# Sums of a graph layer's messages at every second step alone, two rounds in one burst, ahead of the second layer

## The chip, the core and the metric

The kernel runs on one core of a Trainium2 chip. Its five engines matter here: TensorE (PE; its weight loads are shown apart as PEld), VectorE (DVE), ScalarE (ACT), GpSimd (POOL) and SyncE (SP, which issues DMAs). The metric is the time of one execution on the device, in microseconds (us).

## The reference

One message-passing layer of a graph network over 6,250 nodes of 128 features and 100,000 edges, then a layer norm of x plus its result. All numbers are float32.

```python
row, col = (edge_index[0], edge_index[1])            # edges sorted by col
msg_in = jnp.concatenate([node_features[row], node_features[col]], axis=-1)
h = jax.nn.relu(msg_in @ Wm1 + bm1)                  # 256 -> 256
h = jax.nn.relu(h @ Wm2 + bm2)                       # 256 -> 256
messages = h @ Wm3 + bm3                             # 256 -> 128
agg = segment_sum(messages, col); count = segment_sum(1, col)
agg = agg / jnp.clip(count, 1.0)[:, None]
node_in = jnp.concatenate([node_features, agg], axis=-1)
upd = jax.nn.relu(node_in @ Wn1 + bn1) @ Wn2 + bn2
x = _layernorm(x + node_features + upd)
```

## The kernel before

Before the loop, x is multiplied by the upper half of Wm1 into a table in memory (`atab`, a row per node), and its lower half's product becomes another one (`btab`). The 100,000 edges are cut into 196 groups of 512, four tiles of 128 edges each. A loop goes over steps k, one group a step, with these parts:

- `gather` (L533): POOL fetches the rows of `atab` for group k+2 with four indirect DMAs, indices in `srcT`, for odd groups in `srcP`. The `rows` tile has four buffers, so the gather of group g follows the transposes of group g-4. The index copy `pace(k+5)` at the end of an even step (L893, DVE) fills `srcP`, and the odd gather waits for it.
- `first_layer` (L569, L582): PE transposes the gathered rows into two PSUM banks (16 instructions, 64 rows each) and adds the destination's terms by one-hot matmuls. ACT applies bias and relu (L588, four instructions) into `h1`.
- `make_hot` (L547, L552; DVE, even steps): one-hot tables for the next two groups; `oh` places an edge in a window of 32 nodes.
- `second_layer` of group k-1 (L596): 16 PE instructions into two banks, and behind each a DVE instruction (L598) that writes h2. There are six h2 buffers (`x_sb`, `h_more` in the profile).
- `node_step` (L694 to L745): from step 94 on, finished nodes go through the update and the layer norm in pieces, a piece in five stages, one stage a step: PE L700, L715, L719, L727; DVE L694 and L695 (a reciprocal), L702, L704, L706, L730, L734, L735, L741, L743; ACT L722, L737, L745.
- `some_sums` (L604): a one-hot times h2, 32 rows a window, four windows in four column groups of PE at once: one round is eight PE instructions. The last round of a bank is followed by a copy to SBUF on ACT (`part`, L609).
- `turn_sums`: PE turns such a part (L617, three instructions into a bank), DVE loads the windows' first nodes (L627) and adds the windows to the accumulator `acc` in SBUF (L624).

How many tiles share a window differs by region: four tiles in groups 0 to 71 ("quads": four groups to a bank, four rounds), two in groups 72 to 147 ("pairs": two groups, two rounds), one in 148 to 183 ("singles": a group, one round), four again in 184 to 191, two in the last four. `deal` writes down at which step a round is due, the turn one step after the last round.

PSUM has eight banks: seven go round as `bank`, one (`p3`, named `sum_bank`) holds the sums. The order on PE, ACT and DVE is that in which the code is written (a schedule by hand); a wait at the head of an engine's queue holds up all behind it. The loop's body has the parts in this order: first layer, gather, one-hots, second layer of the group before, node stage, turns and adds, sums, and at even steps the index copy.

Of the kernel before, what the change touches and what calls it, by code (L numbers as in the profile page):

```python
# [10 lines left out]
F32 = mybir.dt.float32  # L11
# [9 lines left out]
P = 128  # L21
# [15 lines left out]
def kernel(  # L37
# [39 lines left out]
    H = wm1.shape[1]  # L77
# [4 lines left out]
    NG = -(-E // GE)  # L82
# [16 lines left out]
    GL = NG - 2 * LATE  # L99
# [199 lines left out]
    with tc.tile_pool(name="prep", bufs=1) as prep, tc.tile_pool(name="pp", bufs=3, space=PSUM) as pp, tc.tile_pool(  # L299
        name="pb", bufs=5, space=PSUM  # L300
# [10 lines left out]
        with tc.high_priority():  # L311
# [7 lines left out]
            t = 4  # L319
            for n in (4, 8, 8, 8, 8, 8):  # L320
                n = min(n, NTF - t)
# [193 lines left out]
    with edge, tc.tile_pool(name="wk", bufs=2) as wk, tc.tile_pool(  # L515
        name="banks", bufs=7, space=PSUM
# [7 lines left out]
        def bank():  # L524
            return banks.tile([P, 2, H], F32, name="bank")

        def flat_bank():
            return bank().rearrange("p t h -> p (t h)")
# [16 lines left out]
        def hot_rows(rb):  # L545
            oht = wk.tile([P, 2, HE], BF16, name="oht")
            nc.vector.tensor_scalar(oht, rb, iota_p, None, op0=ALU.is_equal)  # L547
            return oht
# [58 lines left out]
        def part_of(pg, nw):  # L607
            part = wk.tile([P, H + 1], F32, name="part")
            nc.scalar.copy(part[:nw * WN], pg[:nw * WN, :H + 1])  # L609
            return part  # L610
# [26 lines left out]
        def nk_of(g):  # L637
            return 1 if g < 2 * HALVES or g >= GL else 2

        def make_hot(p):  # L640
            ohts[p] = hot_rows(rels[p // 2][:, 2 * (p % 2):2 * (p % 2) + 2])
            make_nodes(p)

        def make_nodes(p):
            ohs[p] = hot_nodes(dloc[:, 2 * p:2 * p + 2, :].rearrange("p g j -> p (g j)"), 2, iota_n)

        def units_of(g):
            q, n = g // 2, wide_of[g]
            tiles = [(ohs[q][:, g % 2, j, :], h2s[g % len(h2s)][:, j, :]) for j in range(NTS[g])]
            return [tiles[j:j + n] for j in range(0, NTS[g], n)]  # L650
# [104 lines left out]
        ohs, ohts, rels = {}, {}, {}  # L755
        rounds, turns_at, added = {}, {}, {}

        def deal(gs, n, steps):

            steps = list(steps)  # L760
            for t, k in enumerate(steps):
                rounds.setdefault(k, []).append((gs, t, n))
            at = steps[-1] + 1
            turns_at.setdefault(at, []).append(gs[0])
            added.update({g: at + 1 for g in gs})

        for r0, r1, n in REGIONS:
            m = min(n, GT)
            for g in range(2 * r0, 2 * r1, m):
                if n == GT:  # L770
                    deal(range(g, g + n), n, (g + 4, g + 5, g + 6, g + 6))
                elif n == 1:
                    deal([g], n, (g + 3,))
                elif r1 == PAIRS:
                    deal(range(g, g + n), n, (g + 3, g + 4))
                elif g + n < NG:
                    deal(range(g, g + n), n, (NG - 1, NG - 1))
        deal([NG - 2], 2, (NG, NG))
        deal([NG - 1], 2, (NG + 1, NG + 1))

        B_STEPS = B_FROM + 2 * (NT - B_EARLY) + 2
        begins, step = {}, B_STEPS
# [7 lines left out]
        sum_banks, parts = {}, {}  # L790

        def some_sums(k):

            for gs, t, n in rounds.pop(k, ()):
                windows = [w for g in gs for w in units_of(g)]
                if t == 0:
                    sum_banks[gs[0]] = flat_bank() if k > NG else p3.tile([P, 2 * H], F32, name="sum_bank")
                sum_tile(sum_banks[gs[0]], windows, t, n)
                if t == n - 1:
                    parts[gs[0]] = part_of(sum_banks.pop(gs[0]), len(windows)), len(windows)  # L800

        def turn_sums(k):
            for g in turns_at.pop(k, ()):
                part, nw = parts.pop(g)
                pt = turned(part, nw)
                add_up(pt, load_bases(uniti[0:1, unit_at[g]:unit_at[g] + nw], nw, ENG.DVE))
# [50 lines left out]
        for g in range(-4, NG + 14, 2):  # L857
            for i in range(g + 4, min(g + 6, NG)):
                terms[i] = fetch(load_bases(tilei[0:1, i * GT:(i + 1) * GT], NTS[i], ENG.SP), nk_of(i))
            if g < -2:  # L860
                continue
            if (g + 2) % 4 == 0 and g + 6 < NG:
                rels[(g + 6) // 4] = places((g + 6) // 4)
            if g < 0:
                continue
            if g == 0:
                first_step()
            for k in (g, g + 1):
                if k < NG:
                    s = st[k] = {}  # L870
                    if k == 1:
                        xts[1] = open_layer(None, NTS[1], xts[1])
                    s["h1"] = first_layer(rows.pop(k, None), terms.pop(k), ohts[k // 2][:, k % 2], NTS[k], nk_of(k),
                                          xts.pop(k, None))
                    if k == 0:
                        next_rows()
                    if k == 2:
                        nc.scalar.copy(*pace(5))
                if 2 * XS <= k + 2 < NG:
                    rows[k + 2] = gather(sources(k + 2))  # L880
                if k % 2 == 0 and k + 2 < NG:
                    make_hot(k // 2 + 1)
                if 0 <= k - 1 < NG:
                    second_layer(st.pop(k - 1)["h1"], h2s[(k - 1) % len(h2s)], NTS[k - 1])
                if k < NG:
                    node_step(k)
                if k <= NG:
                    turn_sums(k)
                some_sums(k)
                if k > NG:  # L890
                    turn_sums(k)
                if k % 2 == 0 and 2 <= k and k + 5 < NG:
                    nc.vector.tensor_copy(*pace(k + 5))  # L893
                if k >= NG:
                    node_step(k)
            if g < 6:
                clear(8)
            if g == 0:
                more_rows()
            t0 = B_EARLY + (g - B_FROM) // 2  # L900
            if g >= B_FROM and (g - B_FROM) % 4 == 0 and t0 < NT:
                pbt = bank()
                for a in range(min(2, NT - t0)):
                    nc.tensor.matmul(pbt[:, a, :], xT[:, (t0 + a) * P:(t0 + a + 1) * P], w1[:, 1, :],  # L904
                                     start=True, stop=True)
                b_terms(t0, pbt, b_rows, b_rest)
            if g == 18:
                late_weights()
            if g == 60:
                made_weights()  # L910
            if g == NG + 2:
                with tc.high_priority():
                    again = nc.values_load(
                        again_i[0:1, 0:1], min_val=0, max_val=1,
                        skip_runtime_bounds_check_because="0 or 1, by its computation")
# [77 lines left out]
```

## Time and profile before

| | |
|---|---|
| runs of the kernel before | 1333.75, 1343.81, 1348.66 us; median 1343.81 |
| the profiled execution | 1338.36 us, span 1336.6 us, TensorE clock 0.981 |
| PE busy | 1236.1 us, 92% of the span |
| DVE, ACT, POOL busy | 618.2 (46%), 441.9 (33%), 748.7 us (56%) |
| L596 on PE | 768.7 us in 3128 instructions |
| L604 on PE | 104.1 + 59.1 us in 1044 + 512 instructions |
| L617 on PE, L624 on DVE | 47.3 us in 291, 96.7 us in 382 |

In the profile a group's row has: line, engine, operation, output<-inputs, count | busy time, mean ns of one | idle time of the engine just before them and what ended it ("issue": nothing that the trace shows). A timeline's row has: start, length (of so many instructions one after the other), engine, line, operation, and in brackets the idle time before it. Starts of one engine's successive rows, taken from each other, give a price that holds the overlap between instructions.

### The profile page before, as it was taken

How to read it: one execution, taken by the hardware profiler on the slowest of the kernel's cores; microseconds unless marked ns; L12 is line 12 of the kernel's file. 1: busy time of each engine (PE TensorE's matmuls, PEld its weight loads, DVE VectorE, ACT ScalarE, POOL GpSimd, SP SyncE). 2: the span in 40 equal slices, each digit the busy share in tenths (PEclk: the TensorE clock that was granted, in tenths of full speed). 3: DMA queues.
4: the chain of work that ended last, by engine and by line, in shares of the span. 5: the costliest groups of instructions: out<-in, count | busy, mean ns of one | idle time of the engine just before them, and what ended most of it. 6: DMA issues, size and time to landing. Idle time of an engine off the chain costs nothing.

```text
span 1336.6 us, 27771 instructions
## 1 busy us (share of the span) xinstructions
PE 1236.1 (92%) x10031; PEld 925.5 (69%) x10032; DVE 618.2 (46%) x1551; ACT 441.9 (33%) x1102; POOL 748.7 (56%) x795
## 2 busy tenths in 40 slices
PE   9779998998999999999899999999999999999997
PEld 7556666666666666676677777777777777777675
DVE  6443333433334333434466554444445556556553
ACT  4432323323323323333333423333233333333331
POOL 2366665665665666656555465565655555555550
PEclk9879999999999999999999999999999999999998
DMA  8544434444434434434444344444444434443330
GB/s 287 177 125 134 132 108 127 130 115 129 133 106 128 135 107 125 134 106 131 126 118 119 114 125 128 118 120 129 118 118 118 115 109 118 109 123 110 106 91 4
DMA packets 107617, 163.90 MB, mean 123 GB/s; under 512 B 26367, under 2 KB 71549, under 8 KB 107457
## 3 DMA queue, kind: packets, MB, share of 16 engines
q0 software_dynamic: 37504, 102.29, 27.7%
q1 hardware_dynamic: 69425, 59.50, 14.0%
q8 instruction: 82, 1.34, 0.4%
q14 instruction: 62, 0.51, 0.1%
q10 hardware_dynamic: 544, 0.26, 0.1%
HBM read 142.48 MB, written 19.86 MB: 121 GB/s over the span
## 4 chain that ended last, share of the span: by engine, by line
PE 89%; issue 7%; DVE 2%; another core or an unknown queue 1%; DMA 1%; ACT 0%; SPq 0%; DVEq 0%
PE bank L596 54%; PE bank L569 9%; PE sum_bank L604 9%; PE bank L582 4%; PE bank L617 2%; PE pbt L431 2%; PE bank L727 2%; PE bank L700 2%; PE bank L719 2%; PE bank L715 2%; PE bank L904 1%; PE pt L448 0%; DVE acc L660 0%; DVE x_sb L598 0%
## 5 line engine op out<-in xcount | busy, mean ns | idle before, releaser
L596 PE MATMUL bank<-w,h 128*128 128x256 f32 x3128 | 768.7, 392 | 67.2 <-issue 64.6
L596 PEld LDWEIGHTS bank<-w,h 128*128 128x128 f32 x3128 | 581.7, 192 | 212.3 <-issue 131.1
L533 POOL DMA_INDIRECT rows<-atab,srcT x392 | 374.9, 956 | 260.6 <-issue 90.4
L533 POOL DMA_INDIRECT rows<-atab,srcP x384 | 364.2, 949 | 277.9 <-issue 126.5
L588 ACT ACTIVATE h<-bank,b 128x256 f32<-128x256 f32 x782 | 306.5, 476 | 395.6 <-remote 189.3
L598 DVE TENSOR_TENSOR x_sb<-bank,nb 128x512 f32<-128x512 f32 x263 | 181.0, 691 | 401.7 <-PE bank L596 233.7
L598 DVE TENSOR_TENSOR h_more<-bank,nb 128x512 f32<-128x512 f32 x128 | 88.3, 692 | 177.5 <-PE bank L596 75.0
L569 PEld LDWEIGHTS bank<-ident,rows 64*128 64x128 f32 x3096 | 112.7, 140 | 77.7 <-issue 56.8
L569 PE MATMUL bank<-ident,rows 64*128 64x64 f32 x3096 | 139.3, 230 | 0.0
L624 DVE TENSOR_TENSOR acc<-acc,bank 128x96 f32 x382 | 96.7, 253 | 51.7 <-PE bank L569 16.5
L604 PE MATMUL sum_bank<-x_sb,oh 128*32 128x257 f32 x1044 | 104.1, 393 | 3.0 <-issue 1.6
L609 ACT COPY part<-sum_bank 128x257 f32<-128x257 f32 x96 | 35.8, 373 | 197.0 <-PE bank L582 75.4
L582 PE MATMUL bank<-oht,terms 64*128 64x128 bf16 (+1 forms) x1132 | 82.6, 237 | 14.5 <-issue 10.9
L604 PE MATMUL sum_bank<-h_more,oh 128*32 128x257 f32 x512 | 59.1, 391 | 1.2 <-DVE h_more L598 0.6
L604 PEld LDWEIGHTS sum_bank<-x_sb,oh 128*32 128x32 f32 x1044 | 28.1, 108 | 41.7 <-issue 34.1
L582 PEld LDWEIGHTS <-terms 64*128 64x128 bf16 x1132 | 44.1, 97 | 16.1 <-issue 13.8
L617 PE MATMUL bank<-ident,part 128*128 128x128 f32 (+1 forms) x291 | 47.3, 271 | 0.5 <-ACT part L609 0.5
L745 ACT ACTIVATE y<-y,sh,rs 128x128 f32<-128x128 f32 (+3 forms) x50 | 22.1, 487 | 67.0 <-DVE sh L743 26.6
L695 DVE RECIPROCAL x_sb<-x_sb 128x256 f32<-128x256 f32 (+3 forms) x26 | 43.0, 1655 | 0.9
L617 PEld LDWEIGHTS bank<-ident,part 128*128 128x128 f32 (+1 forms) x291 | 36.6, 139 | 9.3 <-ACT part L609 1.0
L552 DVE TENSOR_TENSOR oh<-iota_n,dloc 128x256 f32<-128x256 f32 x98 | 40.8, 417 | 3.6 <-ACT dloc L838 3.6
L737 ACT ACTIVATE sd<-mv,eps 128x2 f32<-128x2 f32 (+3 forms) x26 | 7.7, 295 | 97.6 <-DVE mv L735 49.5
(157 smaller groups left out, 625.0 us busy)
## 6 DMA issues: line engine op xcount, KB each, us to landing
terms<-btab SPq DMA_DIRECT2D x566, 32.0 KB
places<-reltab SPq DMA_DIRECT2D x98, 128.0 KB
btab<-x_sb SPq DMA_DIRECT2D x10, 768.0 KB
rows<-atab,srcT POOLq DMA_INDIRECT x392
atab<-acc SPq DMA_DIRECT2D x12, 512.0 KB
rows<-atab,srcP POOLq DMA_INDIRECT x384
xr<-in_x_dram SPq DMA_DIRECT2D x23, 128.0 KB
out_dram<-y SPq DMA_DIRECT2D x23, 128.0 KB
```

The costliest lines, as they stand in the source:

```text
L533: nc.gpsimd.indirect_dma_start(out=ag[:, j, :], out_offset=None, in_=atab[:, :], in_offset=bass.IndirectOffsetOnAxis(ap=idx[:, j:j + 1], a ...
L552: nc.vector.tensor_tensor(oh[:, :ng].rearrange("p g j n -> p (g j) n"), iota.to_broadcast([P, ng * GT, WN]), dl.rearrange("p (j o) -> p j ...
L569: nc.tensor.matmul(ph[h][:, c, u * NQ:(u + 1) * NQ], ag[halves[h], u, c * P:(c + 1) * P], ident[halves[h], halves[h]], is_transpose=True, ...
L582: nc.tensor.matmul(ph[h][:, c, k * n:(k + 1) * n], bw[halves[h], k, c * P:(c + 1) * P], oht[halves[h], k * n:(k + 1) * n], start=False, st ...
L588: nc.scalar.activation(h1[:, c, h * HE:(h + 1) * HE], ph[h][:, c, :], AF.Relu, bias=b1[:, c:c + 1])
L596: nc.tensor.matmul(ph2[:, j - j0, :], h1[:, c, j * P:(j + 1) * P], w2[:, c, :], start=(c == 0), stop=(c == HC - 1))
L598: nc.vector.tensor_tensor(h2[:, j0:j0 + 2, :H], ph2, nb2.to_broadcast([P, 2, H]), op=ALU.max)
L604: nc.tensor.matmul(pg[w * WN:(w + 1) * WN, :H + 1], oh, h2, start=(t == 0), stop=(t == total - 1), skip_group_check=True)
L609: nc.scalar.copy(part[:nw * WN], pg[:nw * WN, :H + 1])
L617: nc.tensor.matmul(pt[:, c, :q], rows, ident[:q, :q], is_transpose=True, start=True, stop=True, skip_group_check=True)
L624: nc.vector.tensor_add(window, window, pt[:, :, j * WN:(j + 1) * WN])
L695: nc.vector.reciprocal(rc, rc)
```

## The change

Three things change. The due steps of the rounds: in quads the four rounds move from steps g+4, g+5, g+6, g+6 to g+5, g+5, g+7, g+7 (in the late quads g+5, g+5, g+6, g+6); in pairs both are at g+3; in singles an even group's round stays at g+3, an odd group's comes a step earlier, so that two singles are summed at the same odd step. The second of these takes one of the seven `bank`s ("beside") where all singles had `sum_bank`, as does the last group of all. And turns with their adds, then sums, stand ahead of the second layer and the node stage of the step.

```diff
-        def deal(gs, n, steps):
+        def deal(gs, n, steps, beside=False):
...
-                rounds.setdefault(k, []).append((gs, t, n))
+                rounds.setdefault(k, []).append((gs, t, n, beside))
...
                 if n == GT:
-                    deal(range(g, g + n), n, (g + 4, g + 5, g + 6, g + 6))
+                    deal(range(g, g + n), n, (g + 5, g + 5, g + 7, g + 7) if g < GL else (g + 5, g + 5, g + 6, g + 6))
                 elif n == 1:
-                    deal([g], n, (g + 3,))
+                    deal([g], n, (g + 3 - g % 2,), g % 2 == 1)
                 elif r1 == PAIRS:
-                    deal(range(g, g + n), n, (g + 3, g + 4))
+                    deal(range(g, g + n), n, (g + 3, g + 3))
...
-        deal([NG - 1], 2, (NG + 1, NG + 1))
+        deal([NG - 1], 2, (NG + 1, NG + 1), True)
...
-                    sum_banks[gs[0]] = flat_bank() if k > NG else p3.tile([P, 2 * H], F32, name="sum_bank")
+                    sum_banks[gs[0]] = flat_bank() if beside else p3.tile([P, 2 * H], F32, name="sum_bank")
...
+                if k <= NG:
+                    turn_sums(k)
+                some_sums(k)
                 if 0 <= k - 1 < NG:
                     second_layer(st.pop(k - 1)["h1"], h2s[(k - 1) % len(h2s)], NTS[k - 1])
                 if k < NG:
                     node_step(k)
-                if k <= NG:
-                    turn_sums(k)
-                some_sums(k)
```

On PE, in the singles at steps 164 and 165, this stood in a row before (x8 behind L596 and x4 behind L604 count written matmuls, each two instructions in the profile; `sum_bank` and `bank` are PSUM banks, `h_more` and `x_sb` are h2):

```order
L596 MATMUL bank<-w_151,h_13544 128x256 x8
L715 MATMUL bank<-xT,wu_159 128x2x2x64 x2
L719 MATMUL bank<-x_sb,wu_159 128x256 x2
L617 MATMUL bank<-ident,part 128x128 x3
L604 MATMUL sum_bank<-h_more,oh 32x257 x4
L569 MATMUL bank<-ident,rows 128x64 x16
L582 LDWEIGHTS terms
L582 MATMUL bank<-oht,terms 128x128
...
L596 MATMUL bank<-w_151,h_13650 128x256 x8
L727 MATMUL bank<-wu_160,x_sb 128x128 x4
L617 MATMUL bank<-ident,part 128x128 x3
L604 MATMUL sum_bank<-x_sb,oh 32x257 x4
```

Now, at steps 163 and 164:

```order
L604 MATMUL sum_bank<-h_more,oh 32x257 x4
L604 MATMUL bank<-h_more,oh 32x257 x4
L596 MATMUL bank<-w_151,h_13474 128x256 x8
L715 MATMUL bank<-xT,wu_159 128x2x2x64 x2
L719 MATMUL bank<-x_sb,wu_159 128x256 x2
L569 MATMUL bank<-ident,rows 128x64 x16
L582 LDWEIGHTS terms
L582 MATMUL bank<-oht,terms 128x128
...
L617 MATMUL bank<-ident,part 128x128 x6
L596 MATMUL bank<-w_151,h_13567 128x256 x8
L727 MATMUL bank<-wu_160,x_sb 128x128 x4
```

Two bursts of one round have become one burst of two, ahead of L596 at the odd step; both turns stand ahead of L596 at the even step. The whole order has 175 bursts of L604 before and 99 now: 18 fewer in the first quads, 38 in the pairs, 18 in the singles, 2 in the late quads.

On DVE, in the singles, an even step before (step 164; the index copy L893 is its last instruction, the four pairs of an ISA register instruction and an addition are cut to one):

```order
L598 TENSOR_TENSOR x_sb<-bank,nb_155 128x2x256 x2
L706 SCALAR_TENSOR_TENSOR xr<-xr,bu_161 128x256
L627 TENSOR_LOAD starts_i
L624 ISA
L624 TENSOR_TENSOR acc<-acc,bank 128x3x32
...
L893 COPY srcP<-srcT 128x4
```

And now, where eight additions are cut to two:

```order
L547 TENSOR_SCALAR oht<-places,iota_p 128x512
L552 TENSOR_TENSOR oh<-iota_n,dloc 128x256
L627 TENSOR_LOAD starts_i
L624 ISA
L624 TENSOR_TENSOR acc<-acc,bank 128x3x32
...
L598 TENSOR_TENSOR x_sb<-bank,nb_155 128x2x256 x2
L730 TENSOR_TENSOR y<-xr,bank 128x256
L734 BN_STATS stats<-y 128x6
L735 BN_AGGR mv<-stats 128x2
...
L893 COPY srcP<-srcT 128x4
```

The additions have moved from behind the node stage, next to L893, to the front of the step, ahead of L598; L893 follows L598 and what the node stage of the step issues. The odd step's additions are gone.

More of the change, by code (lines that the diff above doesn't have):

```diff
@@ L792, in some_sums @@
         def some_sums(k):
-            for gs, t, n in rounds.pop(k, ()):
+            for gs, t, n, beside in rounds.pop(k, ()):
                 windows = [w for g in gs for w in units_of(g)]
                 if t == 0:
-                    sum_banks[gs[0]] = flat_bank() if k > NG else p3.tile([P, 2 * H], F32, name="sum_bank")
+                    sum_banks[gs[0]] = flat_bank() if beside else p3.tile([P, 2 * H], F32, name="sum_bank")
                 sum_tile(sum_banks[gs[0]], windows, t, n)
```

## The prediction

> **What bounds the kernel now.** I read the page first: busy shares, the chain that ended last, the costliest groups.
>
> ```profile
> PE 1236.1 (92%) x10031; PEld 925.5 (69%) x10032; DVE 618.2 (46%) x1551; ACT 441.9 (33%) x1102; POOL 748.7 (56%) x795
> ...
> PE 89%; issue 7%; DVE 2%; another core or an unknown queue 1%; DMA 1%; ACT 0%; SPq 0%; DVEq 0%
> ...
> L596 PE MATMUL bank<-w,h 128*128 128x256 f32 x3128 | 768.7, 392 | 67.2 <-issue 64.6
> ```
>
> TensorE works 1236.1 of 1336.6 us, and 67.2 us of its idle time lies in front of the second layer, L596. That looks like a kernel bound by PE alone. The windows by stage show that it is not so everywhere. The columns are span, PE, weight loads, DVE, ACT and POOL, each with its count.
>
> ```profile
> 300.00:500.00 200.00, 187.01 (x1477) 132.52 (x1476) 74.58 (x163) 62.81 (x153) 122.55 (x130) 0.99 0.42 123
> 712.00:768.00 56.00, 54.08 (x464) 43.01 (x463) 32.95 (x89) 20.80 (x56) 28.73 (x32) 1.00 0.41 118
> 768.00:985.00 217.00, 204.14 (x1802) 157.74 (x1802) 104.40 (x259) 69.40 (x182) 129.21 (x136) 1.00 0.44 122
> 1040.00:1290.00 250.00, 235.85 (x2017) 184.67 (x2015) 139.33 (x377) 85.07 (x225) 142.53 (x151) 1.00 0.40 112
> ```
>
> A gather is four DMA_INDIRECT on POOL, so 300 to 500 us holds 130/4 = 32.5 gathers, 6.15 us each; 712 to 768 us holds 8, 7.0 us each; 768 to 985 us holds 34, 6.38 us each; 1040 to 1290 us holds 37.75, 6.62 us each. The third view asks what POOL waited for, by stage: even groups gather with srcT, odd ones with srcP.
>
> ```profile
> L533 POOL DMA_INDIRECT rows<-atab,srcT x66 | 62.6, 949 | 38.7 <-issue 15.2 <-remote 11.7 <-PE bank L596 10.4
> L533 POOL DMA_INDIRECT rows<-atab,srcP x64 | 60.5, 946 | 39.0 <-issue 14.6 <-remote 12.8 <-PE bank L596 10.0
> ...
> L533 POOL DMA_INDIRECT rows<-atab,srcT x31 | 29.4, 947 | 18.8 <-issue 7.3 <-PE bank L582 4.8 <-DVE x_sb L702 3.4
> L533 POOL DMA_INDIRECT rows<-atab,srcP x30 | 28.4, 945 | 32.8 <-issue 21.4 <-PE bank L582 11.3
> ...
> L533 POOL DMA_INDIRECT rows<-atab,srcT x76 | 72.0, 948 | 45.5 <-issue 17.4 <-PE bank L596 9.7 <-PE bank L582 9.5
> L533 POOL DMA_INDIRECT rows<-atab,srcP x75 | 71.4, 952 | 62.2 <-issue 37.9 <-PE bank L596 15.9 <-PE bank L582 5.0
> ```
>
> The first pair is 300 to 500 us, the second 660 to 768, the third 1040 to 1290. Idle time per gather: 38.7/16.5 = 2.35 and 39.0/16 = 2.44 us in the first; 18.8/7.75 = 2.43 and 32.8/7.5 = 4.37 in the second; 45.5/19 = 2.39 and 62.2/18.75 = 3.32 in the third. About 2.4 us is there whatever the stage; with 3.8 us of work it gives a floor of some 6.15 us a group. So POOL sets the pace in the early stage (PE has 6% to spare), PE in 712 to 768 us (54.08/56 = 96.6% busy), and in the last one neither: PE is 94.3% busy, and the odd gathers come 0.9 us late. The timeline there says why.
>
> ```profile
> 1086.88 0.69 DVE L598 TENSOR_TENSOR x_sb<-bank,nb 128x512 f32<-128x512 f32 x1 [0.96 <-issue]
> 1087.49 0.42 DVE L706 SCALAR_TENSOR_TENSOR xr<-xr,bu 128x256 f32<-128x256 f32 x1
> ...
> 1088.41 0.49 PE L617 MATMUL bank<-ident,part 128*128 128x128 f32 x3
> ...
> 1089.03 0.95 POOL L533 DMA_INDIRECT rows<-atab,srcT  x1 [0.30 <-issue]
> ...
> 1091.29 0.25 PE L582 MATMUL bank<-oht,terms 64*128 64x128 bf16 x2 [1.01 <-issue]
> ...
> 1091.30 1.13 DVE L624 TENSOR_TENSOR acc<-acc,bank 128x96 f32 x4 [3.40 <-PE bank L569]
> ...
> 1092.35 0.17 DVE L893 COPY srcP<-srcT 128x4 int32<-128x4 int32 x1
> 1093.26 0.94 POOL L533 DMA_INDIRECT rows<-atab,srcP  x1 [3.28 <-issue]
> ```
>
> The odd gather at 1093.26 waits for the copy L893, which stands in DVE's queue behind the four adds L624; these stood 3.40 us, though their turn L617 on PE was through by 1088.9. DVE saw that release at 1091.30, 1.3 us after the last DMA_INDIRECT of the running gather (1089.03 + 0.95).
>
> **The change part by part.** *Fewer bursts of sums.* The order has 76 fewer bursts of L604 (18 in the first quads, 38 in pairs, 18 in singles, 2 in the late quads); the matmuls are as many. What one burst costs by being alone:
>
> ```profile
> 581.74 3.72 PE L596 MATMUL bank<-w,h 128*128 128x256 f32 x16
> 585.39 0.64 PE L604 MATMUL sum_bank<-x_sb,oh 128*32 128x257 f32 x8
> 585.96 0.71 PE L569 MATMUL bank<-ident,rows 64*128 64x64 f32 x16
> ...
> 586.82 3.72 PE L596 MATMUL bank<-w,h 128*128 128x256 f32 x16
> 590.38 0.49 PE L617 MATMUL bank<-ident,part 128*128 128x128 f32 x3
> ...
> 521.06 0.41 PE L604 MATMUL sum_bank<-x_sb,oh 128*32 128x257 f32 x2
> ...
> 522.07 0.71 PE L569 MATMUL bank<-ident,rows 64*128 64x64 f32 x16
> ```
>
> From the start of L596 to the next start is 3.65 us where L604 follows and 3.56 where L617 does: entering L604's 128*32 tiling costs 0.09. One round from its start to L569 is 0.57 us; two rounds are 1.01, so a round inside a burst takes 0.44 and leaving costs 0.13. A merge takes away one entry and one exit and leaves one direct change from L596 to L569 instead: between 0.09 + 0.13 - 0.13 and 0.09 + 0.13, that is 0.09 to 0.22. I take 0.13. The new place, between L582 and L596, adds no change beyond these: over two steps there were six changes of tiling and there are now five. For the price of entering from L582's tiling no row exists; 0 to 0.13 by the rows above, which the interval holds.
>
> The Trainium skill, "TensorEngine Tiling (Array Packing)", Key Properties, says that changing the tiling mode drains TensorE, as these rows show with 0.09 and 0.13. Taken with 92% busy it would give all 76 merges to the time, 76 x 0.13 = 9.9 us. The rows of POOL speak against that: the merges before about 660 us, and those of 768 to 985 us, lie where the gathers' cadence is the limit.
>
> So I count the eight pairs of 660 to 768 us and the 18 of the singles: 26 x 0.13 = 3.4 us. The other 50 (6.5 us of PE work) are hidden by the gathers; if that cover were gone they would add 6.5.
>
> *Turns and adds at even steps only, ahead of L596 and L598.* In the singles L893 no longer stands behind adds that wait for a turn of the same step's end: now it follows L598 and a short node stage (L702 and L704, or L730 to L735), and the 1.75 us reciprocal with its stage goes to the odd steps. In the rows above L893 started 4.86 us after L706 did (1087.49 to 1092.35); what is left in that place is a few node instructions of the size of L706's 0.42. The prize is the odd lateness, (3.32 - 2.44) x 18.75 = 16.5 us in 1040 to 1290 us. PE's own time caps it: 250 - 235.85 = 14.15 us of idle. The lower value is what PE's best stage keeps, 96.6%: 235.85/0.966 = 244.2, a gain of 5.8. I take 12, nearer to the cap because the lateness exceeds it, and keep 0 to 14 for the range, 0 because L598 itself can be late (below). In 660 to 768 us L893 still follows the same node work with the reciprocal, in both orders; PE idles only 1.92 us in 712 to 768. I take 1 us.
>
> *What the adds now stand in front of.* At an even step of these stages DVE has L547, L552, then four adds (pairs) or eight (singles), and only then L598, for which the next odd step's sums wait on PE, and behind those L596. The adds' price:
>
> ```profile
> L624 DVE TENSOR_TENSOR acc<-acc,bank 128x96 f32 x382 | 96.7, 253 | 51.7 <-PE bank L569 16.5
> ```
>
> Four are 1.13 us by the row at 1091.30 (1.01 by this mean), eight 2.3. If PE's release of the turn is seen at once, they are done before the first half of L596 (half of 3.56) or little after, and DVE catches up before the second: cost 0. I take 0; the other end is the second rival. Nothing else is queued on SP or POOL past these moves; the gathers and table loads keep their places.
>
> Sum: 3.4 + 12 + 1 = 16.4 us off the profiled execution's 1338.36, that is 1322.0. The median of the runs, 1343.81, stands 5.45 above that execution; on its scale the forecast is 1327.4, or 1.2% less.
>
> **The rivals.** *Hidden.* The late stage's L893 was late because DVE sees PE's releases late, not because of its place: L598 and L702 hang on the same releases. Then only the 3.4 us, or less, come through: 1340. For it: the even gathers, which need no copy, idle 2.39 us anyway. Against: only the odd ones lose 0.9 us more. Chance 0.28.
>
> *The sums wait for L598.* This is the slower one. Rows of a step where PE's releases were seen late:
>
> ```profile
> 609.15 0.38 PE L582 MATMUL bank<-oht,terms 64*128 64x256 bf16 x4
> 609.46 3.72 PE L596 MATMUL bank<-w,h 128*128 128x256 f32 x16
> ...
> 611.34 0.95 POOL L533 DMA_INDIRECT rows<-atab,srcT  x1 [0.30 <-issue]
> ...
> 613.49 1.57 ACT L588 ACTIVATE h<-bank,b 128x256 f32<-128x256 f32 x4 [3.49 <-PE bank L596]
> 613.56 1.41 DVE L598 TENSOR_TENSOR h_more<-bank,nb 128x512 f32<-128x512 f32 x2 [3.26 <-PE bank L617]
> 613.62 0.95 POOL L533 DMA_INDIRECT rows<-atab,srcP  x1 [1.32 <-PE bank L617]
> ```
>
> ACT, DVE and POOL all go on together 1.2 us after the gather's end (611.34 + 0.95), L588 a full 4.0 us after the end of L582, and both halves of L598 together. Before, the sums came a step's work later and the adds behind L598; now, in pairs and singles, the second round wants an h2 that is written 1.41 us after such a release, 0.84 more than the first round covers (0.57), and the adds of the even step may lie ahead of it, 1.1 or 2.3 us. PE's spare time per two steps is (217 - 204.14)/17 = 0.76 us in the pairs and 14.15/18.9 = 0.75 in the singles; above that a wait lengthens the step. With half the adds in the way, at every second of the 38 + 18 odd steps: 19 x (0.84 + 0.55 - 0.76) + 9 x (0.84 + 1.15 - 0.75) = 12.0 + 11.2 = 23.2 us; less 3.4 it is 1343.8 + 19.8 = 1363.6. With the release seen late and no adds in the way it is about nothing. Against it: while POOL sets the pace PE only loses what it would have waited anyway. Chance 0.24.
>
> *Banks.* Beside the node stages', two steps of the singles take eleven banks from the seven in place of ten, so a bank comes round after 7/5.5 = 1.27 steps in place of 7/5 = 1.40: 0.13 x 6.62 = 0.84 us less to empty it. If that were the limit, it would cost up to 18 x 0.84 = 15 us against the 12 hoped for; about 1343. The Trainium skill, "Perfetto Trace Analysis", Optimization Strategy, says that the same gap repeating on the engine that should be saturated can mean too little SBUF or PSUM for the next tile. PE's gap ahead of L596 would fit that, but the rows at 613.5 show the releases arriving with the gather's end and not with the emptying. Chance 0.06, with the first rival's outcome.
>
> That the change does not do what it says is ruled out by the order: bursts and adds stand as announced.
>
> **How the numbers follow.** The forecast has 0.42, its own range 1318 to 1336 (from 26 merges at 0.09 with 5.8, to the cap of 14.15 with 26 at 0.22 and some of the hidden merges). The first and the bank rival have 0.34 at 1336 to 1346, the slower one 0.24 from 1347 up. A measurement of this kernel tells about 1%, 13.4 us, from no change. Faster by over 1% (under 1330.4) are four in five of the forecast's cases, 0.34, and 0.06 where hidden merges show as well, taken from the others: 0.40. Slower by over 1% (over 1357.2) is nearly all of the slower rival: 0.21. Within 1% is the rest, 0.39. The range begins at 1311, with the cap, all merges at 0.22 and the 1.92 us (14.15 + 16.7 + 1.9 = 32.8), and ends at 1360, which leaves out the dearer half of the slower rival and little else: two in ten.
>
> **What would show it.** In 1040 to 1290 us the srcP rows' idle time per gather falls from 3.32 to about 2.5, and L893 no longer shows a wait for L569 or L617 ahead of it; PE is then over 96% busy there. The period before 660 us stays at 6.15 us a gather with PE less busy. L604's group shows no idle ahead of it. I am wrong if L604 shows tens of us of idle released by DVE (the second rival), if srcP's idle stays above 3, or if L598 stands behind L624 and starts late.

## The result, and the profile after

The changed kernel takes 1390.27 us (median; 1387.35 to 1393.78), the kernel before on the same chip 1341.88: a ratio of 1.036 with an interval of 1.030 to 1.043. The forecast was 1327.4, faster by 1.2%; the range ended at 1360. The profiled execution took 1389.14 us.

The page of the changed kernel: busy shares, chain, and the groups of PE that changed (busy time, mean ns | idle ahead, releaser).

```profile
PE 1257.0 (91%) x10031; PEld 950.5 (69%) x10032; DVE 604.9 (44%) x1551; ACT 434.5 (31%) x1102; POOL 750.5 (54%) x795
...
PE 84%; issue 8%; DVE 4%; another core or an unknown queue 2%; ACT 1%; DMA 1%; DVEq 0%; SPq 0%; ACTq 0%
...
L596 PE MATMUL bank<-w,h 128*128 128x256 f32 x3128 | 748.6, 391 | 23.7 <-issue 21.1
...
L569 PE MATMUL bank<-ident,rows 64*128 64x64 f32 x3096 | 147.8, 232 | 23.6 <-issue 23.5
L604 PE MATMUL sum_bank<-x_sb,oh 128*32 128x257 f32 x952 | 108.6, 390 | 24.4 <-issue 16.6
...
L604 PE MATMUL sum_bank<-h_more,oh 128*32 128x257 f32 x464 | 58.9, 396 | 12.7 <-issue 8.0
...
L700 PE MATMUL bank<-acc,w 128*128 128x256 f32 (+3 forms) x104 | 28.1, 395 | 17.0 <-DVE acc L624 12.3
```

The same groups of the kernel before, those that the prediction did not show:

```profile
L569 PE MATMUL bank<-ident,rows 64*128 64x64 f32 x3096 | 139.3, 230 | 0.0
L604 PE MATMUL sum_bank<-x_sb,oh 128*32 128x257 f32 x1044 | 104.1, 393 | 3.0 <-issue 1.6 <-DVE x_sb L598 1.2
...
L604 PE MATMUL sum_bank<-h_more,oh 128*32 128x257 f32 x512 | 59.1, 391 | 1.2 <-DVE h_more L598 0.6 <-issue 0.5
...
L700 PE MATMUL bank<-acc,w 128*128 128x256 f32 (+3 forms) x104 | 25.9, 371 | 1.8 <-issue 1.0 <-DVE acc L624 0.9
```

PE's waits have moved. Ahead of L596 they fall from 67.2 to 23.7 us; ahead of L604 they rise from 4.2 to 37.1, ahead of L569 from nothing to 23.6, ahead of L700 from 1.8 to 17.0. DVE has come onto the chain (2% to 4%). PE's busy time rose as well, by 20.9 us for the same 10031 instructions, and its granted clock was 0.971 in place of 0.981. Why is not shown; a lower clock alone is not the loss, for one of the kernels below ran at 0.964 and took 0.994 of the time of the kernel before.

Where the time went is seen from the start of a group's first DMA_INDIRECT in both timelines:

| group | 74 | 98 | 114 | 146 | 186 | end of span |
|---|---|---|---|---|---|---|
| before, us | 495.3 | 645.2 | 760.5 | 963.5 | 1234.0 | 1336.6 |
| changed, us | 501.0 | 660.7 | 777.3 | 995.2 | 1280.9 | 1387.4 |
| later by | 5.7 | 15.5 | 16.8 | 31.7 | 46.9 | 50.8 |

Most of it is lost from group 114 on. The windows of the changed kernel there, and POOL's groups in 1040 to 1290 us:

```profile
768.00:985.00 217.00, 200.20 (x1704) 153.29 (x1700) 96.91 (x248) 67.21 (x178) 122.61 (x129) 1.00 0.42 117
...
1040.00:1290.00 250.00, 226.48 (x1932) 178.06 (x1933) 127.80 (x347) 77.62 (x211) 131.09 (x138) 0.99 0.39 107
```

```profile
L533 POOL DMA_INDIRECT rows<-atab,srcP x69 | 65.9, 955 | 78.9 <-issue 47.2 <-PE bank L604 27.1 <-PE sum_bank L604 2.6
L533 POOL DMA_INDIRECT rows<-atab,srcT x69 | 65.3, 947 | 40.2 <-issue 15.5 <-PE bank L617 11.3 <-PE bank L596 9.8
```

In 1040 to 1290 us 34.5 gathers run where 37.75 did, PE is 90.6% busy in place of 94.3%, and an odd gather idles 78.9/17.25 = 4.57 us in place of 3.32, an even one 40.2/17.25 = 2.33 in place of 2.39. The forecast had the odd ones at 2.5. From group 114 to 185 the odd gathers' extra idle time is nearly all of the loss: ahead of a gather's first DMA_INDIRECT the odd ones stand 2.56 us in place of 1.61 in groups 114 to 145, and 3.41 in place of 2.60 in groups 146 to 185; 16 x 0.95 + 20 x 0.81 = 31 us, against 30 lost there. In groups 74 to 113, where 11 us are lost, it is the even ones that stand longer (1.93 us in place of 1.52); their part of it was not followed further. The timeline of the changed kernel in the singles shows what L893 waits for now.

```profile
1121.07 0.94 POOL L533 DMA_INDIRECT rows<-atab,srcT  x1 [1.58 <-PE bank L582]
1121.20 1.13 DVE L624 TENSOR_TENSOR acc<-acc,bank 128x96 f32 x4 [1.28 <-PE bank L582]
1121.33 3.62 PE L596 MATMUL bank<-w,h 128*128 128x256 f32 x16
...
1122.70 1.12 DVE L624 TENSOR_TENSOR acc<-acc,bank 128x96 f32 x4 [0.37 <-issue]
...
1124.81 0.95 POOL L533 DMA_INDIRECT rows<-atab,srcT  x1 [0.30 <-issue]
...
1125.77 0.98 PE L569 MATMUL bank<-ident,rows 64*128 64x64 f32 x16
1125.84 0.69 DVE L598 TENSOR_TENSOR x_sb<-bank,nb 128x512 f32<-128x512 f32 x1 [2.02 <-PE bank L727]
...
1127.27 0.42 PE L582 MATMUL bank<-oht,terms 64*128 64x128 bf16 x8 [0.52 <-issue]
1127.36 0.69 DVE L598 TENSOR_TENSOR x_sb<-bank,nb 128x512 f32<-128x512 f32 x1 [0.82 <-PE bank L569]
...
1127.97 0.41 DVE L730 TENSOR_TENSOR y<-xr,bank 128x256 f32<-128x256 f32 x1
...
1129.32 0.17 DVE L893 COPY srcP<-srcT 128x4 int32<-128x4 int32 x1
...
1130.22 0.94 POOL L533 DMA_INDIRECT rows<-atab,srcP  x1 [4.46 <-issue]
```

A release is the signal by which one engine lets a waiting one go on. The adds are done at 1123.8. L598's second half, of an L596 that PE had finished by 1124.95, starts at 1127.36, 1.6 us after the gather's end (1124.81 + 0.95). Behind it stand L730 to L735, then L893, then the gather. The even step's copy waits for the end of the gather that runs, and from there it is another 2.9 us, DVE's work and the copy's own way to POOL, until the odd gather starts: every second gather is late.

### The profile page after: what moved, and what is told of

Read it like the earlier page. It is cut to its first block, busy times and chain, and to the rows that moved or that the text cites. A ratio compares the mean times of both kernels' runs of the same rounds, so it can differ in the third digit from the quotient of the medians.

```text
span 1387.4 us, 27724 instructions
## 1 busy us (share of the span) xinstructions
PE 1257.0 (91%) x10031; PEld 950.5 (69%) x10032; DVE 604.9 (44%) x1551; ACT 434.5 (31%) x1102; POOL 750.5 (54%) x795
## 4 chain that ended last, share of the span: by engine, by line
PE 84%; issue 8%; DVE 4%; another core or an unknown queue 2%; ACT 1%; DMA 1%; DVEq 0%; SPq 0%; ACTq 0%
PE bank L596 49%; PE bank L569 9%; PE sum_bank L604 8%; PE bank L617 4%; PE bank L582 4%; PE bank L700 2%; PE bank L727 2%; PE pbt L431 2%; PE bank L719 2%; PE bank L715 2%; PE bank L904 1%; DVE acc L624 1%; DVE x_sb L598 1%; PE bank L604 1%
## 5 line engine op out<-in xcount | busy, mean ns | idle before, releaser
L596 PE MATMUL bank<-w,h 128*128 128x256 f32 x3128 | 748.6, 391 | 23.7 <-issue 21.1
L596 PEld LDWEIGHTS bank<-w,h 128*128 128x128 f32 x3128 | 590.2, 194 | 158.8 <-issue 73.5
L588 ACT ACTIVATE h<-bank,b 128x256 f32<-128x256 f32 x782 | 305.9, 474 | 517.8 <-remote 221.5
L598 DVE TENSOR_TENSOR x_sb<-bank,nb 128x512 f32<-128x512 f32 x263 | 179.6, 690 | 439.0 <-PE bank L596 191.2
L598 DVE TENSOR_TENSOR h_more<-bank,nb 128x512 f32<-128x512 f32 x128 | 86.8, 689 | 215.5 <-PE bank L596 76.2
L569 PEld LDWEIGHTS bank<-ident,rows 64*128 64x128 f32 x3096 | 117.2, 141 | 88.7 <-issue 77.9
L569 PE MATMUL bank<-ident,rows 64*128 64x64 f32 x3096 | 147.8, 232 | 23.6 <-issue 23.5
L604 PE MATMUL sum_bank<-x_sb,oh 128*32 128x257 f32 x952 | 108.6, 390 | 24.4 <-issue 16.6
L582 PE MATMUL bank<-oht,terms 64*128 64x128 bf16 (+1 forms) x1132 | 82.1, 240 | 10.4 <-issue 8.9
L604 PEld LDWEIGHTS sum_bank<-x_sb,oh 128*32 128x32 f32 x952 | 36.1, 109 | 65.6 <-issue 37.3
L604 PE MATMUL sum_bank<-h_more,oh 128*32 128x257 f32 x464 | 58.9, 396 | 12.7 <-issue 8.0
L582 PEld LDWEIGHTS <-terms 64*128 64x128 bf16 x1132 | 43.1, 98 | 13.0 <-issue 11.2
L722 ACT ACTIVATE x_sb<-bank,bu 128x256 f32<-128x256 f32 (+3 forms) x52 | 21.0, 454 | 80.7 <-PE bank L719 49.7
L609 ACT COPY part<-sum_bank 128x257 f32<-128x257 f32 x78 | 30.2, 387 | 48.3 <-remote 42.2
L700 PE MATMUL bank<-acc,w 128*128 128x256 f32 (+3 forms) x104 | 28.1, 395 | 17.0 <-DVE acc L624 12.3
L695 DVE RECIPROCAL x_sb<-x_sb 128x256 f32<-128x256 f32 (+3 forms) x26 | 43.0, 1656 | 0.9
L617 PEld LDWEIGHTS bank<-ident,part 128*128 128x128 f32 (+1 forms) x291 | 31.1, 143 | 17.8 <-issue 10.2
```

Of the source, the lines that this page charges most:

```text
L569: nc.tensor.matmul(ph[h][:, c, u * NQ:(u + 1) * NQ], ag[halves[h], u, c * P:(c + 1) * P], ident[halves[h], halves[h]], is_transpose=True, ...
L582: nc.tensor.matmul(ph[h][:, c, k * n:(k + 1) * n], bw[halves[h], k, c * P:(c + 1) * P], oht[halves[h], k * n:(k + 1) * n], start=False, st ...
L588: nc.scalar.activation(h1[:, c, h * HE:(h + 1) * HE], ph[h][:, c, :], AF.Relu, bias=b1[:, c:c + 1])
L596: nc.tensor.matmul(ph2[:, j - j0, :], h1[:, c, j * P:(j + 1) * P], w2[:, c, :], start=(c == 0), stop=(c == HC - 1))
L598: nc.vector.tensor_tensor(h2[:, j0:j0 + 2, :H], ph2, nb2.to_broadcast([P, 2, H]), op=ALU.max)
L604: nc.tensor.matmul(pg[w * WN:(w + 1) * WN, :H + 1], oh, h2, start=(t == 0), stop=(t == total - 1), skip_group_check=True)
```

## The experiments

Each kernel was timed beside the kernel before, on the same chip; there were five such comparisons, on five different chips, and ratios are to the kernel before of the same one. A ratio differs somewhat between chips: the changed kernel had 1.036 on the chip of the result and 1.043 in the fourth comparison. Diffs are against the changed kernel where nothing else is said. The kernel before took 1325.65, 1340.81, 1189.94, 1323.74 and 1339.12 us in them; what is behind the third number is told below. In the kernels that move L893 its line is L884 or L885.

### The two parts apart

The merged bursts in the old place, where the last two rounds of the early quads come a step earlier than in the change:

```diff
-                    deal(range(g, g + n), n, (g + 5, g + 5, g + 7, g + 7) if g < GL else (g + 5, g + 5, g + 6, g + 6))
+                    deal(range(g, g + n), n, (g + 5, g + 5, g + 6, g + 6))
...
-                if k <= NG:
-                    turn_sums(k)
-                some_sums(k)
                 if 0 <= k - 1 < NG:
                     second_layer(...)
                 if k < NG:
                     node_step(k)
+                if k <= NG:
+                    turn_sums(k)
+                some_sums(k)
```

> The merged bursts and the bank beside, in the old place: second layer, node stage, turns and adds, sums. (The quads' rounds come at g+5, g+5, g+6, g+6, since at g+7 the first h2 would be overwritten there.) Theory A, that the new place does the harm (adds ahead of L598 on DVE, sums right behind L582 on PE): about the kernel before, 1335 to 1345 us. Theory B, that the merging does it (a pair's two rounds and both singles at one step, the second single's bank): 1370 to 1390.

The new place without the merging:

```diff
-                    deal(range(g, g + n), n, (g + 5, g + 5, g + 7, g + 7) if g < GL else (g + 5, g + 5, g + 6, g + 6))
+                    deal(range(g, g + n), n, (g + 5, g + 6, g + 7, g + 7) if g < GL else (g + 5, g + 5, g + 6, g + 6))
-                    deal([g], n, (g + 3 - g % 2,), g % 2 == 1)
+                    deal([g], n, (g + 3,))
-                    deal(range(g, g + n), n, (g + 3, g + 3))
+                    deal(range(g, g + n), n, (g + 3, g + 4))
```

> The new place alone: turns and sums ahead of the second layer and the node stage, with the rounds spread as before (quads g+5, g+6, g+7, g+7, because g+4 is too early there; pairs g+3, g+4; each single g+3 in the sum bank). Theory A: 1375 to 1395 us. Theory B: 1340 to 1355.

Measured: merged bursts alone 1.049 (1.045 to 1.053), the new place alone 1.043 (1.038 to 1.049). Each fits one of the two theories, so neither theory is the whole: either part alone costs as much as both. A cause that fits this is something that the place and the number of bursts both touch.

### Turns and adds back; L893 at the head

```diff
-                if k <= NG:
-                    turn_sums(k)
                 some_sums(k)
                 if 0 <= k - 1 < NG:
                     second_layer(...)
                 if k < NG:
                     node_step(k)
+                if k <= NG:
+                    turn_sums(k)
```

> The changed kernel with the turns and adds back behind the node stage, the sums still ahead of the second layer and merged. Theory A1, that the adds at the head of DVE's queue do most of it (they hold L598, and L700 must wait for them): 1335 to 1355 us, L700's idle back from 17 to about 2 us. Theory A2, that the sums' place does most of it (L604 right behind L582 waits for L598): 1370 to 1390, L604's idle stays near 37 us.

```diff
+                if k % 2 == 0 and 2 <= k and k + 5 < NG:
+                    nc.vector.tensor_copy(*pace(k + 5))
                 if k <= NG:
                     turn_sums(k)
...
-                if k % 2 == 0 and 2 <= k and k + 5 < NG:
-                    nc.vector.tensor_copy(*pace(k + 5))
```

> The changed kernel with the index copy L893 ahead of the adds and of L598 in its even step. If the odd gathers' lateness behind L598 and the node stage sets the time of the late stages: 1345 to 1365 us, srcP's idle per gather in the singles near 2.5 us in place of about 3.7. If PE's own waits set it and the gathers only follow: 1385 to 1395.

Measured: turns and adds back 1.070 (1.063 to 1.077), the worst of all and dearer than either theory had it. L893 at the head 1.021 (1.015 to 1.028): on the chip where merged bursts alone cost 4.9%. POOL's groups of that kernel, 1040 to 1290 us:

```profile
L533 POOL DMA_INDIRECT rows<-atab,srcP x72 | 68.1, 945 | 61.9 <-PE bank L582 33.8 <-issue 16.7 <-PE bank L569 11.3
L533 POOL DMA_INDIRECT rows<-atab,srcT x71 | 68.0, 957 | 56.5 <-PE bank L582 39.0 <-issue 15.9 <-PE bank L617 1.4
```

An odd gather idles 61.9/18 = 3.44 us here, an even one 56.5/17.75 = 3.18, and PE's releases end these waits more than before: the odd ones are no longer far apart from the even ones. The 2.5 expected for the odd ones did not come, because POOL now waits for PE; PE itself is 91.4% busy in that stretch, with waits of its own (below). The worst kernel fits the same reading: with turns back, an even step has L598, the node stage and eight adds ahead of L893, and its odd gathers stand 4.92 us ahead of their first DMA_INDIRECT in groups 146 to 185, the even ones 1.01.

### L893 at the head of the other three, and of the kernel before

The same move was made in the kernel before, in each part alone and in the one with turns and adds back.

> The kernel before with the index copy L893 at the head of its even step on DVE, ahead of L598, the node stage and the adds. Theory C, that where L893 stands in DVE's queue sets the odd gathers and with them the late stages: 1 to 2% faster than the kernel before (its odd gathers idle 2.6 us in groups 146 to 185, even ones 1.5). Theory D, that L893 only matters once PE is out of step: within 1%.

> Merged bursts in the old place, with L893 at the head of its step. Theory C: the 47 us that the merged bursts cost with L893 behind the even step's adds fall to 10 or less (the pairs' and singles' adds have all moved to the even steps, in front of L893). Theory D (PE's own waits and its half-clock windows): 35 us or more stay.

> The new place with the rounds spread as before, and L893 at the head of its step. Theory C: the 38 us that the new place costs fall to 10 or less. Theory D: 30 or more stay.

> Sums merged and ahead of the second layer, turns and adds behind the node stage, L893 at the head. Theory C: the costliest variant (86 us over the kernel before, L893 behind everything) comes down to that of the changed kernel with L893 at the head (15 us) or lower, since L700 no longer waits for adds. Theory D: it stays 50 or more above.

Measured, beside the earlier runs:

| | L893 last in its step | L893 at the head |
|---|---|---|
| kernel before | 1 | 0.988 (0.983 to 0.994) |
| merged bursts, old place | 1.049 (1.045 to 1.053) | 0.994 (0.991 to 0.997) |
| new place, not merged | 1.043 (1.038 to 1.049) | 0.997 (0.994 to 0.999) |
| both, turns and adds behind the node stage | 1.070 (1.063 to 1.077) | 0.999 (0.996 to 1.001) |
| both (the change) | 1.036 (1.030 to 1.043) | 1.021 (1.015 to 1.028) |

In a row the two columns come from different chips; the first four ratios on the right are from one chip. Theory C holds in all of these four: with L893 out of the way either part costs less than 1% (0.994 and 0.997 against 0.988), and 7.1% of the fourth row go. In the kernel before, an even step, where L893 is, has adds only in the singles, four, since the pairs' stand in odd steps; merging brings the pairs' there as well and doubles the singles', and the new place puts adds ahead of L598. For the third row the adds are not all of it: in groups 114 to 145 its even steps have none, and its odd gathers stand 2.57 us all the same. The sums ahead of L596 are a candidate there, not tested; that the cost goes with L893's place is shown. Only the change keeps 2%. Something more is in that row, and the fourth one, in which turns and adds stand behind the node stage, does not have it.

### L700 and its step's adds

The page of the changed kernel showed L700 waiting. It reads the accumulator `acc` that the adds write, and the change puts the adds ahead of it in the same step. With L893 at the head:

```profile
1103.44 1.11 DVE L624 TENSOR_TENSOR acc<-acc,bank 128x96 f32 x4
...
1104.92 1.12 DVE L624 TENSOR_TENSOR acc<-acc,bank 128x96 f32 x4 [0.37 <-issue]
1105.96 1.28 DVE L598 TENSOR_TENSOR h_more<-bank,nb 128x512 f32<-128x512 f32 x2
1106.20 1.10 PE L700 MATMUL bank<-acc,w 128*128 128x256 f32 x4 [2.30 <-DVE acc L624]
```

PE stands 2.30 us until the eighth add is done; over that kernel it is 24.5 us ahead of L700. The change also lets a node stage begin at an odd step (the last round of a pair, and that of an odd single, is due one step earlier), which from step 114 on puts L700 on the even steps. The experiment begins the stages at even steps again:

```diff
             step = max(step, max(added[g] for g in range(min(2 * r, NG))))
+            step += step % 2 if step < NG else 0
```

> The changed kernel with L893 at the head of its step, and every node stage begun at an even step, so that from group 114 on L700 falls on odd steps, where there are no adds. Theory L, that L700's wait for the eight adds of its own step is most of what is left (24.5 us of idle ahead of L700 with L893 at the head): that idle goes to about 2 us and the ratio to the kernel before from 1.021 to 1.003 to 1.010. Theory M, that the wait only moves to L604 or L596: 1.016 or more.

> The changed kernel with L893 at the head and L700 on odd steps. Theory L, where releases come late: 1.003 to 1.010 (1.021 with L700 on even steps), idle ahead of L700 near 2 us. At once: 0.993 as in the third comparison.

> The changed kernel with the node stages begun at even steps (L700 on odd ones from group 114 on) and L893 left where the change has it. With the changed kernel, L893 alone and both, this closes a square. If the two costs add up: the 2.1% that L700's place was worth with L893 at the head come off here too, 1.018 to 1.024 where releases come late. If L893's wait hides L700's: 1.030 or more. Where releases come at once, 0.993 to 0.998.

With L893 at the head the ratio goes from 1.021, in the first comparison, to 1.000 (0.997 to 1.003) in the fourth, and L700's idle to this:

```profile
L700 PE MATMUL bank<-acc,w 128*128 128x256 f32 (+3 forms) x104 | 25.7, 370 | 1.2 <-DVE acc L624 1.2
```

That is theory L, with a ratio even below its 1.003 to 1.010. In the fourth comparison the changed kernel itself was at 1.043 (below), so on one and the same chip the two moves together take away all that the change cost. With L893 left last it is worth nothing: 1.046 (1.039 to 1.053) against 1.036 and, once more, 1.043 (below), although L700's idle is 1.3 us there. The two costs do not add: where L893 makes the gathers late, PE has to wait somewhere, and L700's wait would be inside that; and with the stages on the old parity the reciprocal L695 (1.66 us on DVE at the mean) is in front of L893 again. Which of the two it is was not separated.

### Late releases, and the gathers

In the third comparison (L700 on odd steps, no index copy, and two kernels without gathers) the kernel before itself took 1189.94 us. The cause of that could not be chosen or switched; what the traces show is that there PE's releases reach the other engines at once. The page of the kernel without index copy, from there, and the group that waits for PE's first layer:

```profile
PE 1172.7 (99%) x10031; PEld 915.0 (77%) x10032; DVE 606.9 (51%) x1456; ACT 440.2 (37%) x1101; POOL 751.0 (63%) x795
...
L533 POOL DMA_INDIRECT rows<-atab,srcT x776 | 741.7, 956 | 387.9 <-issue 186.6
L588 ACT ACTIVATE h<-bank,b 128x256 f32<-128x256 f32 x782 | 306.1, 474 | 245.5 <-PE bank L582 234.3
```

A DMA_INDIRECT lasts what it lasted elsewhere (956 ns), PE is 99% busy. From the end of a group's L582 to the start of its L588 it is 0.10 us at the median of the 196 groups there (35 ns at the tenth percentile), 2.2 us in the kernel before as profiled at first.

> The kernel before with no index copy at all: odd groups gather with srcT like the even ones, as early as the rows buffers allow. If the copy only delays: 0.983 to 0.990 of the kernel before, as with the copy at the head. If holding the odd gathers back serves something (DMA, releases): 1.00 or more.

> The kernel before without the index copy. Where releases come late, and if the copy only delays: 0.983 to 0.990, as with the copy at the head of its step (0.988); if it serves something there, 1.00 or more. Where they come at once: 1.000, as in the third comparison.

The kernel before without the index copy: 1.000 (0.999 to 1.001) there, 0.986 (0.980 to 0.992) in the fifth comparison, where releases came late. So the copy delays and serves nothing that these runs show. Where releases come late, leaving it out and moving it to the head (0.988) are the fastest versions found that compute the whole, and their intervals overlap; where they come at once it is the changed kernel with both moves (below).

> The kernel before with the gathers of the first six groups only; later groups compute on the rows that lie in the four buffers, so that part is left out. Theory N, that PE's releases come late because of the running gathers: ACT L588 starts within 0.3 us of the end of L582 and PE sets the pace, 1250 to 1300 us. Theory O, that they come late for a reason of PE's own: L588 still starts microseconds after L582, 1310 or more.

> The changed kernel with the same gathers left out. Theory N: what the merged bursts save shows in the time, 76 x 0.13 = 10 us or up to 15 less than the kernel before without gathers. If the new order's own waits (L604 for L598, L700 for the adds) do not need the gathers: no gain, or slower by 10 us and more.

> The kernel before with the first six groups' gathers only. Theory N, where releases come late otherwise: here they come at once, 1185 to 1215 us. Theory O (not the gathers' doing): within 3% of the kernel before, L588 still 2 us and more behind L582. Where releases come at once anyway: the same as the kernel before.

> The changed kernel without gathers. Theory N: 1185 to 1220 us and within 1% of the kernel before without gathers, wherever it runs. Theory O: 2% or more slower than that one where releases come late.

```diff
-                    rows[k + 2] = gather(sources(k + 2))
+                    rows[k + 2] = kept[k % 4] = gather(sources(k + 2)) if k < 4 else kept[k % 4]
```

In the third comparison the gathers cost nothing (0.999, 0.998 to 1.000), and so theories N and O could not be told apart there. In the fourth, where they are 9% of the time, the kernel before without them took 1200.97 us (0.908, 0.902 to 0.914) and the changed one 1202.65 (0.910, 0.905 to 0.916). Of the former, in the fourth comparison, a step on PE and ACT, and ACT's group:

```profile
962.05 0.39 PE L582 MATMUL bank<-oht,terms 64*128 64x128 bf16 x8
...
962.37 3.72 PE L596 MATMUL bank<-w,h 128*128 128x256 f32 x16
962.47 1.57 ACT L588 ACTIVATE h<-bank,b 128x256 f32<-128x256 f32 x4 [0.40 <-PE bank L582]
...
L588 ACT ACTIVATE h<-bank,b 128x256 f32<-128x256 f32 x782 | 306.7, 475 | 254.1 <-PE bank L582 243.4
```

L588 starts 0.03 us after L582 here, and 0.09 us at the median of all groups. Without gathers the lateness is gone: theory N. What about a gather does it, the instructions on POOL, the transfers or the waiting for rows to land, was not separated, since all three went at once. Why gathers do so on four of these five chips (medians of 1.4 to 2.1 us in their traces of kernels with gathers) and not on the fifth is open.

The two kernels without gathers also show what the merged bursts are worth to PE. In the third comparison, before and changed:

```profile
PE 1172.9 (99%) x10031; PEld 915.0 (77%) x10032; DVE 612.4 (51%) x1551; ACT 441.0 (37%) x1102; POOL 24.6 (2%) x35
```

```profile
PE 1164.7 (98%) x10031; PEld 918.2 (77%) x10032; DVE 605.7 (51%) x1551; ACT 434.3 (36%) x1102; POOL 24.6 (2%) x35
...
L700 PE MATMUL bank<-acc,w 128*128 128x256 f32 (+3 forms) x104 | 26.5, 377 | 11.2 <-DVE acc L624 11.2
```

76 merges save 8.2 us of PE, 0.11 each, and L700's wait takes 11.2 back: 1.004 (1.002 to 1.005). With L893 at the head, L700 on odd steps and all gathers, on that chip, the saving shows in the time: 1182.70 against 1189.94 us, 0.993 (0.992 to 0.995).

### The changed kernel once more

> The changed kernel once more, beside the kernel before. In the third comparison PE's releases came at once in every kernel (L588 0.5 us after L582 at the median, in the first ones 2.5 us), and the kernel before took 1190 us. Theory P, that the change only costs where releases come late: if this chip shows them at once, 0.990 to 1.006 of the kernel before (merges -8 to -10 us, L700's waits +11); if late, 1.03 to 1.045 as at first. Rival Q, that the new order costs by itself: 1.02 or more either way.

This comparison, the fourth, had late releases (1.9 us at the median; the text above has 2.5 and 0.5 for the earlier kernels, where the medians are 2.2 and 0.10): 1.043 (1.035 to 1.050). Theory P and rival Q both allow that, and are not told apart by it. Whether the changed kernel is slower where they come at once was not run with its gathers; without them it was by 0.4%.

## Why the prediction was wrong

The forecast was faster, the outcome slower by 48 us. By its steps:

**The burst's price was right.** 0.09 to 0.22 a merge was given, 0.13 taken; 0.11 was measured. The Trainium skill states ("TensorEngine Tiling (Array Packing)", Key Properties) that a change of the tiling mode drains TensorE. The trace agrees as far as it goes: with 76 bursts fewer PE is busy 8.2 us less. That the gathers' cadence would keep the early merges out of the time is not refuted, but not shown either: on the chip of the result group 74 came 5.7 us later, not earlier.

**The step that failed is the 12 us from L893.** It said of L893 "now it follows L598 and a short node stage" and took that for a place without a wait. But the wait of 3.40 us that was seen there before did not belong to the adds: it was that of DVE for a release of PE while a gather ran. L598's second half is released by PE too, and as late; it had simply stood in front of the adds. The odd gathers' idle rose from 3.32 to 4.57 us in place of falling to 2.5, and from group 114 to 185 the odd gathers stood 31 us longer where 12 us were to be won. The row for it was quoted in the prediction: at 613.56 both halves of L598 started together, after the gather's end. It served the second rival and the lower end of this term, which stopped at 0; that the term could turn its sign was not seen. Putting L893 at the head is what shows the step: 1.021 in place of the 1.036 and 1.043 of the change, and 1.000 with L700's wait out of the way too.

**The pairs were left out of that step.** From group 114 to 145 L893 had no adds in its step before, and odd gathers stood no longer than even ones (1.61 and 1.60 us). Now all the adds there are in even steps. The table of L893's place shows the merging by itself, pairs and singles together: merged bursts in the old place, 1.049 and 0.994.

**L700 was not seen.** The list of who waits for the adds named L598 and L604 and not the node stage's read of `acc`, L700 on PE: 17.0 us of idle in the changed kernel, and with L893 at the head the difference between 1.021 and 1.000, taken on two chips.

**The second rival had the sign and, in part, the way.** Two of the signs that were named for being wrong came: srcP's idle stayed above 3, and L604 showed tens of us of idle, though the view by lines puts only 5.5 + 4.7 = 10.2 of them to DVE. The rival put the release of L598 behind the gather's end and priced PE's wait at L604: +19.8 us, where 48 came. L604's idle did rise by 33 us, but L596's fell by 43.5 at the same time; the wait had in good part changed its place. What lengthened the late stages was what stood behind L598 on DVE.

**Hidden, and banks.** The first rival's reason, that DVE sees PE late whatever L893's place, was half of the cause; it lacked that the change puts L893 behind more of such waits. The bank beside does not make the loss: merged bursts with that bank are at 0.994 when L893 is at the head. The Trainium skill ("Perfetto Trace Analysis", Optimization Strategy) says that a repeated gap can mean too little SBUF or PSUM for the next tile. It did not bear here: with the same buffers and all gathers PE is 99% busy on the chip where releases come at once.

**The floor of 6.15 us a group** was taken for a property of the gather. Of it 5.0 us are the gather's own (4 x 0.95 + 4 x 0.30), the rest is waiting: where releases came at once, more than a third of the gathers of the kernel without index copy followed the one before within 5.2 us, the fastest in 5.0.

## What to carry to other kernels

Before an instruction is moved behind another one on an in-order engine, ask of each instruction that will stand ahead of it what releases it and when that release is seen, not how long it works: here a copy of 0.17 us behind the wrong neighbour cost 5% (1.049 against 0.994). A small instruction on which another engine's start hangs belongs at the head of its step, or should not be there at all. And list all readers of what a moved instruction writes, also those of another stage; L700 was one.

## What the runs showed of the hardware

While gathers run (four DMA_INDIRECT from POOL), PE's releases can reach ACT, DVE and POOL as late as 1.2 to 1.6 us after the gather's last one; all that the gathers cost the kernel before was 1323.74 - 1200.97 = 123 us on a chip with late releases, and nothing on the one without. A ratio from one chip can therefore miss what a change is worth: with L893 at the head and L700 on odd steps the changed kernel is at 1.000 where releases come late and at 0.993 where they come at once.
